# Node tiles in fours, and some gathered rows replaced by columns that VectorE copies, in a two-layer graph network

## The chip, the cores and the metric

The kernel runs on one core of a Trainium2 chip. The metric is device time in microseconds (us) of one execution. PE is TensorE, DVE is VectorE, ACT is ScalarE, POOL is GpSimd and SP is SyncE; PEld is PE's weight load. L12 is line 12 of the kernel that a profile belongs to, so the numbers before and after the change differ.

## The reference

There are 12500 nodes of 128 features and 200000 edges, sorted by destination. `src` is random.

```python
h = jnp.maximum(_layernorm(x, axis=-1), 0.0)
w = edge_weight_raw / jnp.maximum(wsum, EPS)[dst]      # wsum: sum of weights at the edge's destination
feat = jax.nn.relu(h @ W_pool + b_pool)
msg = feat[src] * w[:, None]
neigh = jax.ops.segment_max(msg, dst, num_segments=N)  # 0 where a node has no edge
rst = h @ W1_self + neigh @ W1_neigh + b1
h1 = jax.nn.relu(rst / jnp.maximum(jnp.linalg.norm(rst, axis=1, keepdims=True), EPS))
msg2 = h1[src] * w[:, None]
neigh2 = jax.ops.segment_sum(msg2, dst, num_segments=N) / jnp.maximum(deg, 1.0)[:, None]
out = x + jax.nn.relu(h1 @ W2_self + neigh2 @ W2_neigh + b2)
```

So each layer reads one row of a table for each edge, in random order, reduces the rows of a destination (by maximum, then by weighted sum), and puts two 128x128 products behind it at the nodes.

## The kernel before

The edges are worked in 391 groups of 512 (the last has 320), a group in four chunks of 128 edges; the nodes in 98 tiles of 128. A group ends the edges of some 32 nodes, so four groups complete a node tile. The program is straight-line code, and each engine takes its instructions in the order in which the loops write them. A wait holds everything behind it on its engine.

*Prologue* (to about 290 us). Layer norm, the product with `W_pool`, and the table `feat_d` in DRAM. The normalized features also stay on the chip turned, features on partitions and a node in each column: `h0T`, over the first of two wide tiles (`one_way`). Layer 1 leaves its output as rows in the table `h_d` and turned in `h1T`, over the second (`other_way`). The sums or maxima of the neighbours are gathered in the tile that is not read.

*Layer 1* (to about 2420 us) runs over the groups with index `i`, as a pipeline of several stages in each iteration:

- POOL issues four indirect DMAs (`gather`, L507), each of which fetches the 128 rows of a chunk into a ring of buffers. The first 17 groups take another way. Layer 1's ring starts wide and ends, as buffers are needed elsewhere, with the 11 buffers that layer 2 has too.
- PE transposes the chunks into a PSUM tile `pm` (L896, two buffers), so that an edge is a column. DVE multiplies them by the edge weights `gs`, loaded by SP (L940).
- One iteration later DVE runs a scan with maximum along the edges (L911), which starts again at each new destination (by `kt`) and takes the group before it up by `carry`, a copy of the last column (L929). Two instructions (L933, L936) pick one of each pair of columns into `sc`, and two make selection matrices `sel` (L922).
- PE turns `sc` back into rows (L952, tile `pr`), ACT copies them (L906), PE multiplies them by `sel` (L961), which puts each destination's last value into its column of a window of 48 nodes, and ACT copies the window to its place (L849).
- Node tiles (`nodes1`) come one at a time when their groups are done: two PE products (L747 for the node itself, L743 for the neighbours), the bias on DVE (L757), squares and root on ACT, maximum, reciprocal and scaling on DVE (L764, L765, L773), a PE transpose (L780) and a copy by ACT; two tiles share a store to `h_d`. Side jobs fill gaps.

*Layer 2* (to the end) runs over the groups again. In iteration `i` POOL gathers group `i` from `h_d` into one of 11 buffers; DVE makes a matrix `s` with the edges' weights at their destinations (`places` L996, `weighted` L1001); PE multiplies the rows of group `i-1` by it (`window_product`, L1008, four products in eight passes, tile `pa`, three buffers); DVE adds the result of group `i-2` into the window of `agg2` (`window_add`, L1013), at an address held in a register. These registers are loaded eight at a time (L729).

In four of each 16 groups there is a node tile (`nodes2`): PE products L747 (node), L742 (bias) and L743 (neighbours); L743 needs a `window_add`. In the next iteration DVE applies the ReLU and adds `x` (L802). Four tiles share one load of `x` and one store of `out`.

## Time and profile before

| | |
|---|---|
| median of 3 runs | 4619.21 us (4613.98 to 4619.93) |
| the profiled execution | 4650.7 us, its span 4648.7 us |
| granted PE clock, mean | 0.527 |
| prologue, to 290 us | POOL busy 143.69 us, DVE 156.82, PE 148.17, ACT 133.08 |
| layer 1, 290 to 2420 us | POOL 1347.84, DVE 1306.94, PE 981.70, ACT 282.97 |
| layer 2, 2420 to 4648 us | POOL 1461.81, DVE 278.00, PE 865.25, ACT 0.00 |

The share of busy time is read by stage, as the table does it, since the two layers load DVE very differently. A row of a group of instructions gives line, engine, operation, the tiles written and read, the count, the busy time, the mean length in ns, and the idle time of the engine just before them with what ended it. `remote` stands where the profile shows no instruction of this core that ended at that moment; `issue` where nothing was waited for.

### The profile page before, as it was taken

Reading aid. Unit: us, or ns where it says so; the run is one execution under the profiler, and the core shown is the slowest. Engines: PE = TensorE matmul, PEld = TensorE weight load, DVE = VectorE, ACT = ScalarE, POOL = GpSimd, SP = SyncE. Lnnn points to the kernel's source line nnn. Section 1 sums busy time; section 2 is a strip of 40 time slices with the busy share of each in tenths; the row PEclk is TensorE's granted clock in tenths of the full one; section 3 lists DMA queues with packets and bytes.
Section 4 is the critical chain, followed back from the end, with each engine's and each line's share of the span. In section 5 each row is a group of like instructions: output and inputs, shape, how many; then the busy total and the mean of one; then the engine's idle time right before and its main releaser. Section 6 shows DMA issues by size and latency. Waiting matters only on the chain.

```text
span 4648.7 us, 32678 instructions
## 1 busy us (share of the span) xinstructions
PE 1995.1 (43%) x8700; PEld 1817.3 (39%) x8700; DVE 1741.8 (37%) x5165; ACT 416.0 (9%) x1509; POOL 2953.3 (64%) x3143
## 2 busy tenths in 40 slices
PE   3654543444444444444453344334334333334334
PEld 2444433443434343433342334333334333333334
DVE  3676655765666566665560111111101111111111
ACT  3531111111111111111110000000000000000000
POOL 5356666666666666666646666666666666666665
PEclk8665555555555555555555555555555555555555
DMA  4333443444444444444431112112111111211111
GB/s 130 109 114 116 126 117 103 125 117 114 118 115 120 115 117 116 119 116 117 113 100 46 47 47 62 51 50 56 50 52 53 51 52 51 55 51 52 53 54 45
DMA packets 196303, 397.11 MB, mean 85 GB/s; under 512 B 60703, under 2 KB 69790, under 8 KB 196112
## 3 DMA queue, kind: packets, MB, share of 16 engines
q0 software_dynamic: 100032, 204.97, 17.3%
q1 hardware_dynamic: 95344, 189.06, 13.2%
q8 instruction: 73, 1.20, 0.1%
q10 hardware_dynamic: 736, 0.92, 0.1%
q14 instruction: 118, 0.97, 0.1%
HBM read 374.96 MB, written 19.77 MB: 85 GB/s over the span
## 4 chain that ended last, share of the span: by engine, by line
another core or an unknown queue 23%; issue 23%; PE 20%; POOL 19%; DVE 13%; DMA 1%; ACT 1%; POOLq 0%; ACTq 0%; DVEq 0%
POOL gt L507 18%; PE pa L1008 5%; PE pm L896 5%; DVE pm L911 4%; PE pn L961 4%; DVE pm L940 2%; PE pr L952 2%; DVE sc L936 1%; DVE sc L933 1%; DMA gt<-h_d,srcT 1%; DVE sel L922 1%; PE pn L743 1%; PE pf L643 1%; PE pn L780 1%
## 5 line engine op out<-in xcount | busy, mean ns | idle before, releaser
L507 POOL DMA_INDIRECT gt<-h_d,srcT x1551 | 1463.9, 944 | 743.6 <-issue 419.6
L507 POOL DMA_INDIRECT gt<-feat_d,srcT x1303 | 1230.0, 944 | 680.5 <-issue 294.5
L1008 PE MATMUL pa<-s,gt 128*128 128x24 f32 x3102 | 685.3, 382 | 734.4 <-remote 561.1
L1008 PEld LDWEIGHTS pa<-s,gt 128*128 128x128 f32 x3102 | 682.0, 330 | 748.7 <-remote 567.8
L1013 DVE TENSOR_TENSOR way<-pa,way 128x41 f32 x391 | 78.0, 199 | 1866.9 <-remote 1323.6
L896 PE MATMUL pm<-ident,gt 128*128 128x128 f32 (+1 forms) x1303 | 349.7, 423 | 521.5 <-issue 314.3
L940 DVE TENSOR_TENSOR pm<-pm,gs 128x512 f32<-128x512 f32 x390 | 271.1, 695 | 694.6 <-remote 529.1
L911 DVE TENSOR_TENSOR_SCAN pm<-kt,carry,pm 128x512 f32<-128x512 bf16 x389 | 496.3, 1276 | 4.0
L961 PEld LDWEIGHTS pn<-sel,rows 128*128 128x128 f32 x1564 | 368.8, 324 | 230.8 <-ACT way L849 128.2
L896 PEld LDWEIGHTS pm<-ident,gt 128*128 128x128 f32 (+1 forms) x1303 | 235.8, 218 | 560.4 <-issue 338.5
L961 PE MATMUL pn<-sel,rows 128*128 128x48 f32 x1564 | 358.2, 377 | 217.4 <-ACT way L849 121.9
L743 PE MATMUL pn<-w_2n,way 128*128 128x128 f32 x192 | 74.4, 491 | 601.3 <-issue 325.9
L743 PEld LDWEIGHTS pn<-w_2n,way 128*128 128x128 f32 x192 | 52.8, 323 | 620.2 <-issue 406.6
L906 ACT ACTIVATE rows<-pr 128x256 f32<-128x256 f32 x392 | 149.7, 383 | 1532.8 <-remote 662.1
L952 PE MATMUL pr<-ident,sc 128*128 128x128 f32 x782 | 241.8, 411 | 8.0 <-issue 3.9
L922 DVE TENSOR_SCALAR sel<-cols,lastT,invT 128x48 f32<-128x48 f32 x782 | 243.6, 312 | 0.0
L933 DVE COPY sc<-pm 128x256 f32<-128x256 f32 x391 | 162.6, 416 | 109.5 <-remote 85.9
L952 PEld LDWEIGHTS pr<-ident,sc 128*128 128x128 f32 x782 | 167.2, 224 | 11.5 <-issue 6.1
L936 DVE COPY_PREDICATED sc<-kt,pm 128x256 f32<-128x256 int16 x389 | 168.5, 433 | 4.9 <-issue 4.9
L507 POOL DMA_INDIRECT w2T<-feat_d,srcT x100 | 94.3, 943 | 105.8 <-DVE raw_mv L521 52.0
L780 PE MATMUL pn<-ident,h 128*128 128x128 f32 x94 | 41.9, 446 | 236.8 <-DVE ss L765 73.0
L780 PEld LDWEIGHTS pn<-ident,h 128*128 128x128 f32 x94 | 17.3, 184 | 270.1 <-issue 217.2
(273 smaller groups left out, 2079.6 us busy)
## 6 DMA issues: line engine op xcount, KB each, us to landing
gs<-in_edge_weight SPq DMA_DIRECT2D x389, 256.0 KB
kt<-keep_d SPq DMA_DIRECT2D x97, 512.0 KB
gt<-h_d,srcT POOLq DMA_INDIRECT x1551
gt<-feat_d,srcT POOLq DMA_INDIRECT x1303
feat_d<-fr SPq DMA_DIRECT2D x24, 256.0 KB
xr<-in_x SPq DMA_DIRECT2D x24, 256.0 KB
out<-o SPq DMA_DIRECT2D x24, 256.0 KB
h_d<-h SPq DMA_DIRECT2D x47, 128.0 KB
```

What stands on the lines that cost most here:

```text
L507: nc.gpsimd.indirect_dma_start(out=gt[:k, j, :], out_offset=None, in_=table_d[:, :], in_offset=bass.IndirectOffsetOnAxis(ap=srcT[:k, t, j, ...
L743: nc.tensor.matmul(po, nT, W[neigh_w], start=False, stop=True)
L896: nc.tensor.transpose(pms[i][:, j * P:j * P + k], gt[:k, j, :], ident[:k, :k])
L906: nc.scalar.activation(rws[g][:k, j, :], pr[:k, j, :], AF.Copy)
L911: nc.vector.tensor_tensor_scan(pm[:, :ne], kt[:, :ne], pm[:, :ne], carry, op0=OP.add, op1=OP.max)
L922: nc.vector.tensor_scalar(part, cols[:k, 1, :], lastT[:k, t, j, r:r + 1], invT[:k, t, j, r:r + 1], op0=OP.is_equal, op1=OP.mult)
L933: nc.vector.tensor_copy(sc[:, :ne // 2], two[:, :, 1])
L936: nc.vector.copy_predicated(sc[:, :ne // 2], new[:, :, 1], two[:, :, 0])
L940: nc.vector.tensor_tensor(pms[i][:, :n], rows[:, :n], ws.pop(i)[:, :n], OP.mult)
L952: nc.tensor.transpose(prs[g][:k, j, :], sc[:, j * P:j * P + k], ident)
L961: nc.tensor.matmul(pas[g], rows[:k, j, :], sel[:k, j, :], start=j == 0, stop=j == len(chunks) - 1)
L1008: nc.tensor.matmul(pas[g][:, PART_AT[j]:PART_AT[j] + PART], gt[:k, j, :], s[:k, j, :], start=j == len(chunks) - 1, stop=j == 0, skip_group ...
```

## The change

*Node tiles four at a time.* `quad1` takes the place of `nodes1` for the tiles below 92, `quad2` that of `nodes2` for all full fours. The products are made with features on partitions and four tiles side by side (128x512), so that a bias is a column that ACT adds. `quad1` has the squares summed over the features by a product with a matrix of ones; DVE then runs a maximum, a reciprocal and a product over 128x512. The stages stand in consecutive iterations; a quad comes once in 16 groups.

*PSUM and waits in layer 1.* `pm` has three buffers instead of two, the two `pr` buffers share one tile, the carry is read from the old `pm` instead of a copy, and a group's chunks are transposed in reversed order.

*Columns by DVE.* In layer 1 in every eighth group from 33, and in layer 2 in every third from 13, chunk 1 is not gathered. DVE copies the 128 columns of its source nodes from the turned features that are on the chip. The prologue writes each edge's byte address into a table `at_d` in DRAM (one multiplication and one store for each of four tiles of edges, for both layers); SP loads a chunk's list; a TENSOR_LOAD puts 16 addresses into registers (L751), and eight SCALAR_TENSOR_TENSOR (L800) copy two columns each, with both operands addressed by registers. Each pair comes out as the negative of the first column and the second itself. A chunk takes eight such bursts, spread over its eight or three groups. In layer 1 PE multiplies the columns by `W_pool` straight into `pm`, where ACT applies bias and ReLU with the signs. In layer 2 PE transposes the chunk (L1201, `flip`), and ACT copies it back with the signs, into the buffer that a gather would have filled.

```diff
+    def linear_quad(pn, t, agg, self_w, neigh_w):
+        c = slice(t * P, (t + Q) * P)
+        po = flat(pn())
+        nc.tensor.matmul(po, W[self_w], turned_to[self_w][:, c], start=True, stop=False)
+        nc.tensor.matmul(po, W[neigh_w], agg[:, c], start=False, stop=True)
+        return po
+
+    def quad1(wk, pn, t):
+        po = linear_quad(pn, t, agg1, "1s", "1n")
+        yield
+        sq = wk.tile([P, G], F32, name="sq4", bufs=1)
+        hT = wk.tile([P, G], F32, name="hT4", bufs=1)
+        nc.scalar.activation(sq, po, AF.Square, bias=b1_col)
+        nc.scalar.activation(hT, po, AF.Relu, bias=b1_col)
+        yield
+        ss = flat(pn())
+        nc.tensor.matmul(ss, ones_w, sq, start=True, stop=True)
+        yield
+        nc.scalar.activation(sq, ss, AF.Sqrt)
+        yield
+        c = slice(t * P, (t + Q) * P)
+        nc.vector.tensor_scalar(sq, sq, TINY, None, op0=OP.max)
+        nc.vector.reciprocal(sq, sq)
+        nc.vector.tensor_tensor(turned_to["2s"][:, c], hT, sq, OP.mult)
+        yield
+        ph = pn()
+        for q in range(Q):
+            nc.tensor.transpose(ph[:, q, :], strided(turned_to["2s"], t + q, Q), ident)
+        yield
+        h = wk.tile([P, G], F32, name="sq4", bufs=1).rearrange("p (q d) -> p q d", d=D)
+        nc.scalar.activation(h, ph, AF.Copy)
+        nc.sync.dma_start(runs(h_d, t, Q, Q), in_runs(h, Q))
+
+    def quad2(wk, pn, t, xr):
+        po = linear_quad(pn, t, agg2, "2s", "2n")
+        yield
+        oT = wk.tile([P, G], F32, name="oT4", bufs=1)
+        nc.scalar.activation(oT, po, AF.Relu, bias=b2_col)
+        yield
+        pt = pn()
+        for q in range(Q):
+            nc.tensor.transpose(pt[:, q, :], strided(oT, q, Q), ident)
+        yield
+        o = wk.tile([P, Q, D], F32, name="o4", bufs=2)
+        nc.vector.tensor_tensor(o, pt, xr, OP.add)
+        nc.sync.dma_start(runs(out, t, Q, Q), in_runs(o, Q))
...
@@ in sources(), for each of four tiles of edges @@
+            for layer in range(2):
+                row = (layer * NT + t) * P
+                place = wk.tile([P, G], I32, name="sa")
+                nc.vector.tensor_scalar(place, sr[:, t, :], 4.0, float(TABLES_AT[layer]), op0=OP.mult, op1=OP.add)
+                nc.sync.dma_start(at_d[row:row + P, :], place)
+                yield
...
@@ class Columns @@
+            while (g := first + int(len(self.place) * every)) < end:
+                part = len(self.place) * every % 1 if even else 0
+                self.place[g] = len(self.place) % 2
+                span = min(every, within)
+                begin = g - int(span) - lead
+                steps = P // BURST
+                for turn, step in ((begin - 2, self.load), *((g + k, step) for k, step in after)):
+                    self.plan.setdefault(turn, []).append((step, g, 0))
+                for k in range(steps):
+                    turn = begin + int(k * span / steps + part)
+                    self.plan.setdefault(turn, []).append((self.fetch, g, k * BURST))
...
+    def two_by_two(slot, r, columns_read):
+        for e in range(0, BURST, 2):
+            nc.vector.scalar_tensor_tensor(slot[:, r + e:r + e + 2], zero_high, columns_read[e],
+                                           columns_read[e + 1].to_broadcast([P, 2]),
+                                           op0=OP.subtract, op1=OP.min)
...
@@ layer 1 @@
+        for k, engine, copy, j, every, first in ((0, mybir.EngineType.DVE, two_by_two, 1, 8, FIRST + 16),):
...
+            def multiplied(g, _, j=j, slot=slot):
+                nc.tensor.matmul(pms[g][:, j * P:(j + 1) * P], W["pool"], slot(g), start=True, stop=True)
...
-                gts[i] = gather(buffer(i, True), feat_d, i)
+                gts[i] = gather(buffer(i, True), feat_d, i, besides=bycol)
...
-                pms[i] = ps.tile([P, G], F32, name="pm", bufs=2)
+                pms[i] = ps.tile([P, G], F32, name="pm", bufs=3)
...
-                if g + 1 < NG:
-                    carry = wk.tile([P, 1], F32, name="carry")
-                    nc.vector.tensor_copy(carry, pm[:, ne - 1:ne])
+                carry = pm[:, ne - 1:ne]
...
@@ layer 2 @@
+        for k, engine, copy, j, every, first in ((0, mybir.EngineType.DVE, two_by_two, 1, 3, 13),):
...
+            bycol.append(Columns(engine, copy, False if k else None, other_way, 1, lists_of(k), slot,
+                                 ((-2, turned), (0, back)), 4, j, every, first, NG - 5, True, 5))
...
-                gts[i] = gather(buffer(i, False), h_d, i)
+                gts[i] = gather(buffer(i, False), h_d, i, besides=bycol)
                 places(i)
+            for c in bycol[:1]:
+                c.ahead()
+                c.fetch_one(i)
...
+            quad_stage(1)
+            quad_stage(3)
+            for c in bycol[:1]:
+                c.ahead()
+                c.fetch_one(i)
...
                 window_add(g, window_at(mybir.EngineType.DVE, g))
```

On DVE, two consecutive groups in the middle of layer 2 read like this before (`way_64` is `agg2`, `place` the comparison with the places in the window, `s` the weighted matrix):

```order
L1013 ISA
L1013 TENSOR_TENSOR way_64<-pa,way_64 128x41
L996 TENSOR_TENSOR place<-place,locT 128x96
L1001 TENSOR_TENSOR s<-place,w2T 128x96
L1013 ISA
L1013 TENSOR_TENSOR way_64<-pa,way_64 128x41
```

The same engine in the changed kernel, from one window add to the next (`listed` is the list of addresses, `way_66` the turned features, `gt_109` a buffer of the ring; L1214, L1219 and L1231 are the former L996, L1001 and L1013):

```order
L1231 TENSOR_TENSOR way_65<-pa,way_65 128x41
L751 TENSOR_LOAD listed
L800 SCALAR_TENSOR_TENSOR gt_109<-b_80,way_66 128x2 x8
L1214 TENSOR_TENSOR place<-place,locT 128x96
L751 TENSOR_LOAD listed
L800 SCALAR_TENSOR_TENSOR gt_109<-b_80,way_66 128x2 x8
L1219 TENSOR_TENSOR s<-place,w2T 128x96
L751 TENSOR_LOAD listed
L800 SCALAR_TENSOR_TENSOR gt_109<-b_80,way_66 128x2 x8
L844 TENSOR_LOAD bases
L1231 ISA
L1231 TENSOR_TENSOR way_65<-pa,way_65 128x41
```

Between two window adds there are now up to three bursts, each a load and eight copies, all behind the first add and ahead of the second; with eight bursts in three groups, some iterations have two.

On PE, a place in layer 2 where node tiles begin reads like this before (`gt_` buffers of successive groups, `w_2s`, `w_2n` the weights of the layer):

```order
L1008 MATMUL pa<-s,gt_101 128x24 x4
L747 MATMUL pn<-w_2s,way_65 128x128
L742 MATMUL pn<-b_81,ident 128x128
L743 MATMUL pn<-w_2n,way_64 128x128
L1008 MATMUL pa<-s,gt_102 128x24 x4
L747 MATMUL pn<-w_2s,way_65 128x128
L742 MATMUL pn<-b_81,ident 128x128
L743 MATMUL pn<-w_2n,way_64 128x128
L1008 MATMUL pa<-s,gt_103 128x24 x4
```

The same engine at such a place in the changed kernel:

```order
L1201 MATMUL flip<-ident,gt_103 128x128
L905 MATMUL pn<-way_66,w_2s 128x512
L906 MATMUL pn<-way_65,w_2n 128x512
L1226 MATMUL pa<-s,gt_101 128x24 x4
L1226 MATMUL pa<-s,gt_102 128x24 x4
L1226 MATMUL pa<-s,gt_103 128x24 x4
L945 MATMUL pn<-ident,oT_41836 128x128 x4
L1201 MATMUL flip<-ident,gt_106 128x128
L1226 MATMUL pa<-s,gt_104 128x24 x4
```

The products of four tiles stand together ahead of one group's product instead of three by three ahead of four, the transposes of the quad follow three groups later, and in every third group a fetched chunk is turned.

More of the change, by code (lines that the diff above doesn't have):

```diff
@@ L500, in edges_of, with gather @@
         return *divmod(g, P), ne, [(j, min(P, ne - j * P)) for j in range(-(-ne // P))]
-    def gather(gt, table_d, g, only=None, last=None):
+    def gather(gt, table_d, g, only=None, last=None, besides=()):
         t, r, ne, chunks = edges_of(g)
@@ L506, in gather @@
         for j, k in chunks if only is None else chunks[only:only + 1]:
+            if any(c.j == j and c.takes(g) for c in besides):
+                continue
             nc.gpsimd.indirect_dma_start(
@@ L975, in gnn_kernel @@
                 side_step()
+            for c in bycol:
+                c.turn(i, c.load, c.fetch)
         assert not busy
@@ L1079, in gnn_kernel @@
                 window_add(g, window_at(mybir.EngineType.DVE, g))
-        assert late is None
+            for c in bycol[:1]:
+                c.ahead()
+            for c in bycol:
+                c.turn(i, c.turned)
+            for c in bycol[1:]:
+                c.fetch_one(i)
+            for c in bycol:
+                c.turn(i, c.back)
+            for c in bycol:
+                c.turn(i, c.fetch)
+        assert late is None and not quads
     both.close()
```

159 lines of the change are left out of this document (143 added, 16 removed).

## The prediction

> **What bounds the kernel now.** I read the page first (busy shares, chain, costliest groups), then the table of stretches, then one line at a time, then the timeline of one period of layer 2.
>
> ```profile
> PE 1995.1 (43%) x8700; PEld 1817.3 (39%) x8700; DVE 1741.8 (37%) x5165; ACT 416.0 (9%) x1509; POOL 2953.3 (64%) x3143
> another core or an unknown queue 23%; issue 23%; PE 20%; POOL 19%; DVE 13%; DMA 1%; ACT 1%; POOLq 0%; ACTq 0%; DVEq 0%
> L507 POOL DMA_INDIRECT gt<-h_d,srcT x1551 | 1463.9, 944 | 743.6 <-issue 419.6
> L507 POOL DMA_INDIRECT gt<-feat_d,srcT x1303 | 1230.0, 944 | 680.5 <-issue 294.5
> ```
>
> POOL is the busiest engine at 64%, and it does almost nothing but issue gathers: four of 128 rows in each group. The chain of waits ends on no single engine, so POOL is not simply the bound; something also holds it up. The next views are the table of stretches (start and end, length, then busy us and count of PE, PEld, DVE, ACT, POOL) for a middle piece of layer 1 and of layer 2, and POOL's line in the second piece.
>
> ```profile
> 700.00:2200.00 1500.00, 679.91 (x3003) 607.83 (x3003) 916.04 (x2281) 193.33 (x813) 969.30 (x1027) 0.52 0.42 117
> 2500.00:4500.00 2000.00, 780.28 (x3436) 751.67 (x3435) 242.36 (x1159) 0.00 (x0) 1324.86 (x1404) 0.50 0.19 52
> L507 POOL DMA_INDIRECT gt<-h_d,srcT x1404: 938/944/1148, 2503.4 to 4496.8; - x176
>   issue: 380.3, 1243
>   remote: 224.1, 78
> ```
>
> Layer 2 passes 1404 gathers in 2000 us, 1.425 us each, or 5.70 us a group of four; layer 1 1027 in 1500 us, 1.46 each. Of this 0.944 is the gather and 380.3/1243 = 0.31 us the gap that always follows: 1.25 us, 4.99 a group, if nothing stopped it. The rest is some 78 stalls of 3 us, one every 26 us. From the page's two groups, idle less 0.30 for each gather: 743.6 - 465 = 278 us of stalls in layer 2, 680.5 - 391 = 290 us in layer 1. VectorE is busy for 12% of layer 2 and 61% of layer 1.
>
> What stalls POOL shows in the timeline (start, length, engine, line, and in brackets the idle time before) and in the groups of layer 2.
>
> ```profile
> 3262.89 10.41 PE L1008 MATMUL pa<-s,gt 128*128 128x24 f32 x48 [12.12 <-remote]
> 3289.35 0.20 DVE L1013 TENSOR_TENSOR way<-pa,way 128x41 f32 x1 [12.71 <-remote]
> 3289.61 0.84 PE L743 MATMUL pn<-w_2n,way 128*128 128x128 f32 x2 [15.26 <-issue]
> 3262.36 0.94 POOL L507 DMA_INDIRECT gt<-h_d,srcT  x1 [4.48 <-remote]
> 3307.10 0.94 POOL L507 DMA_INDIRECT gt<-h_d,srcT  x1 [5.12 <-remote]
> 3308.32 0.20 DVE L1013 TENSOR_TENSOR way<-pa,way 128x41 f32 x1 [18.30 <-remote]
> 3319.36 0.94 POOL L507 DMA_INDIRECT gt<-h_d,srcT  x1 [2.50 <-PE pn L742]
> L1013 DVE TENSOR_TENSOR way<-pa,way 128x41 f32 x354 | 70.6, 199 | 1682.4 <-remote 1220.1 <-PE pa L1008 279.8 <-issue 117.3
> L1008 PE MATMUL pa<-s,gt 128*128 128x24 f32 x2806 | 619.8, 382 | 639.9 <-remote 521.3 <-issue 60.4 <-DVE s L1001 30.6
> L743 PE MATMUL pn<-w_2n,way 128*128 128x128 f32 x174 | 68.0, 494 | 566.1 <-issue 320.8 <-DVE way L1013 192.9 <-DMA gt<-h_d,srcT 52.4
> ```
>
> PE's products of the first row end at 3273.3, yet VectorE's window add L1013, which needs the last of them, starts at 3289.35, sixteen us later, while POOL issues without a break; the next comes 1.2 us after a POOL stall of 5.12. So VectorE learns late that PE is done, mostly when POOL pauses. PE, in step with VectorE, then frees the ring of 11 buffers in batches (48 products = six groups in 10.4 us), and POOL stops when the ring is full. Node tiles make it worse: L743 needs VectorE's add, and VectorE's next add needs PE again. PE's idle time before L743 is 566 us against 640 before L1008, though node tiles come in only 4 of 16 groups. In this period of 16 groups POOL stalls 4.2, 4.8 and 2.2 us beyond its gap, the last two, 63%, among the four node tiles.
>
> **The change, part by part.** The sum is against the profiled execution's own 4650.7 us, which is 0.7% above the median of 4619.21 (ratio 0.9932).
>
> *Gathers removed.* Layer 1 has columns in groups 33, 41 ... 385 (45), layer 2 in 13, 16 ... 385 (125): 170 of POOL's 3143 instructions. At POOL's undisturbed 1.25 us: layer 2 **-156**, layer 1 **-56**. If POOL's pace of 1.43 holds in proportion it is -179 and -66; if the ring's consumer sets the pace, 0 and 0. I take 1.25, the part that POOL certainly no longer spends.
>
> *Node tiles by four, layer 2.* Four round trips L743 - L1013 in 16 groups become one, spread over four iterations. The stalls at stake are 63% of 278 = 175 us; none may go, since the stall before 3262.36 came without a node tile. I take 40%, **-70** (0 to -175): the other late signals stay and will refill some of it.
>
> *Layer 1: tiles by four, a third `pm` buffer, no carry copy.*
>
> ```profile
> L757 DVE TENSOR_TENSOR r<-pn,b 128x128 f32<-128x128 f32 x64 | 17.9, 280 | 0.0
> L773 DVE TENSOR_SCALAR h<-r,ss 128x128 f32<-128x128 f32 x66 | 19.5, 295 | 2.3
> L765 DVE RECIPROCAL ss<-ss 128x1 f32<-128x1 f32 x66 | 10.8, 164 | 2.3
> L764 DVE TENSOR_SCALAR ss<-ss 128x1 f32<-128x1 f32 x66 | 9.9, 150 | 0.0
> L338 DVE RECIPROCAL r_f<-r_f x4: 952/953/954, 135.1 to 739.4; 128x128 f32<-128x128 f32 x4
> L940 DVE TENSOR_TENSOR pm<-pm,gs 128x512 f32<-128x512 f32 x260 | 180.9, 696 | 502.5 <-remote 398.7 <-PE pm L896 30.8 <-issue 26.6
> L929 DVE COPY carry<-pm 128x1 f32<-128x1 f32 x261 | 42.6, 163 | 0.0
> ```
>
> VectorE gave four tiles 4 x (280 + 295 + 164 + 150) = 3.56 us. A quad's reciprocal of 128x512 is four of L338's, 3.8 us, and the maximum and product some 0.7 each as L940: 5.2 us, or 1.6 more in 16 groups. The carry copy gives back 16 x 0.07 (what its successor starts later), 1.1. VectorE waits 502.5 us before L940 in this piece, about 31 in 16 groups, which covers it; were it uncovered, 23 quads would cost 23 x 5.2 = 120. Of the 290 us of stalls the shorter round trips may take some: **-30**, a tenth (-290 to +120). The chunk straight into `pm` swaps a transpose for a product of the same size, and its two ReLUs go to ScalarE, busy for 13% here: 0.
>
> *VectorE's fetch.* A chunk is 8 loads of 16 registers and 64 SCALAR_TENSOR_TENSOR of 128x2.
>
> ```profile
> L729 DVEq TENSOR_LOAD <-bases x49: 593/596/1056, 2430.3 to 4625.9; - x49
> L1041 DVEq TENSOR_LOAD <-bases x3: 308/309/314, 2543.4 to 2755.5; - x3
> 161.94 0.16 DVE L530 SCALAR_TENSOR_TENSOR raw_off<-raw_mv,raw_rstd 128x4 f32<-128x4 f32 x1
> 162.02 0.28 DVE L520 BATCH_NORM_STATS2 raw_st<-gt 128x6 f32<-128x128 f32 x1
> L802 DVE SCALAR_TENSOR_TENSOR o<-pn,xr 128x128 f32<-128x128 f32 x86 | 24.2, 281 | 0.0
> 3263.07 0.27 DVE L996 TENSOR_TENSOR place<-place,locT 128x96 f32<-128x96 f32 x1 [0.17 <-issue]
> 3263.66 0.27 DVE L996 TENSOR_TENSOR place<-place,locT 128x96 f32<-128x96 f32 x1
> ```
>
> Eight registers take 596 ns, one 309: 41 ns for each further one, so 16 take 0.92 us (two loads of eight, 1.19, is the upper end). The nearest small instruction, L530, lets its successor start after 80 ns; L802, much larger, takes 281. I take 80, as the sizes 128x4 and 128x2 are close: a burst is 0.92 + 8 x 0.08 = 1.56 us, a chunk **12.5 us** (at 281 ns and nothing overlapped 8 x (0.92 + 2.25) = 25.3; at 80 ns with loads wholly under other work 5.1). VectorE's own work in a group of layer 2 is 0.59 us (the two L996 rows), 1.8 in three. So three groups need 14.3 us of VectorE, 13.7 of POOL's bare issuing (11 x 1.25), and passed in 17.1 until now. That fits, but tightly.
>
> The bursts stand in the in-order queue behind L1013 that waits for PE. In the time in which VectorE now sits there (1682 of 2000 us), the work behind it is not done, and after the signal it has 14.3 us to catch up with in three groups instead of 1.8. PE's products, and POOL through the ring, wait for that. The nearest row gives only bounds: 0 if a burst ahead of L1013 fills the wait, hundreds of us if the waits add (third rival). I take **+40**, a fifth of the 208 us of layer 2's stalls left above. In layer 1 a burst goes into each of eight groups with its load behind the scan (L1111), which is long enough (1.28 us) to hide it; eight instructions of 0.08 to 0.13 are some 1 us on a VectorE with 2.2 us free in a group: 0.
>
> A rule of the Trainium skill speaks against this part. Its page "Runtime: NRT & Kernel Launch", section "Instruction fetch mechanics", puts a register load at about 200 ns per register even in bulk. By it 16 registers take 3.2 us, a chunk 30.7, and layer 2 is bound by VectorE at about 10.8 us a group, +1.9 ms by that estimate. L729 against L1041 says 41 ns, and the measurement decides.
>
> *The rest.* The flip transpose and its copy (125 products of L743's size, 0.49 us, on a PE that is idle for 61% of layer 2; ScalarE has nothing else there) come two groups ahead of use: 0, or 125 x 0.49 = 61 uncovered. SP's 170 list loads are issued two groups before the first burst, behind stores of tiles on the same queue: 0 as long as such a store waits under 10 us. The address lists in the prologue, 8 multiplications of 128x512 at some 0.69 (as L940) and 8 stores beside other work: **+5** (0 to 20).
>
> **Sum:** -156 - 56 - 70 - 30 + 40 + 5 = -267; 4650.7 - 267 = 4384, times 0.9932 = **4354 us**. Layer 2 would pass at 5.70 - 186/391 = 5.22 us a group.
>
> **Rivals.**
> 1. *The gathers were hidden.* PE's idle time before L1008 is put to `remote` and VectorE, none of it to a landing gather, so data are there when PE comes, and the pace may be that of the exchange between PE and VectorE. Then only -70 - 30 + 5 remain: 4556, **4525 us**. Against it: POOL itself fills 1.25 of 1.43 us, and signals are late just while it issues. Chance 0.17.
> 2. *The stalls of layer 2 go altogether,* as VectorE is no longer parked and PE's round trips are spread. The floor is then VectorE's 14.3 us in three groups, 4.77 each: 0.93 x 375 = -349, with layer 1's -86 and +5: 4221, **4192 us**. For it: most stalls of the period shown lie at the node tiles. Against: the one before 3262.36 does not. Chance 0.14.
> 3. *VectorE becomes the bound of layer 2: slower.* Point of decision: a burst above (17.1 - 1.8)/8 = 1.91 us. If each fetching instruction holds the queue for 199 ns, as the register-addressed L1013 is long, a burst is 2.51, three groups 21.9, a group 7.30: +1.60 x 375 = +600, with -86 and +5: 5170, **5135 us**. For it: no row shows these instructions in a row, and L1013's address comes from a register too. Against: L530's 80 ns. Chance 0.11.
> 4. *Each register costs a load of its own,* 309 ns as L1041: 4.94 us for 16, (8 x (4.94 + 0.64) + 1.8)/3 = 15.5 us a group, +9.8 x 375, some **8.2 ms**. Only if L729's 596 for eight does not go on to sixteen. Chance 0.01. The figure of the Trainium skill's page "Runtime: NRT & Kernel Launch", weighed above, would lie between L729 and this.
>
> **How the numbers follow.** The forecast has 0.57, its own range 4230 to 4460 (-70 and -30 each from nothing to double, the fetch 0 to +100). With rivals 1 and 2 the range is **4150 to 4550**; rivals 3 and 4 and the tails stay out. A measurement of this kernel can tell about 0.2% from no change. Faster by more: forecast and rivals 1 and 2 but for their tails, 0.86; within 0.2%: 0.02; slower: 0.12.
>
> **What would show it.** Burst: spacing of L800 and the length of L751 (0.92 expected). POOL: L525 in layer 2 at 1.33 us each and fewer `remote` stalls; at 1.43 with 11 gathers rival 1 is out too, as the pace is then POOL's own. Node tiles: PE's idle before the quad's products well under the 566 us of L743. Rival 3 shows as a VectorE that is busy or loading throughout layer 2 and POOL stalling for most of its time. I would be most wrong if VectorE's wait at L1231 and its bursts add up instead of overlapping.

## The result

The changed kernel takes 4667.4 us (4643.06 to 4677.91, 6 runs) where the kernel before takes 4619.57: ratio **1.0103** (1.0082 to 1.0124), slower by 1.0%. The forecast was 4354 us, the range 4150 to 4550. Its profiled execution took 4670.77 us, its span 4669.0. First the page's rows of the changed kernel.

```profile
PE 2045.8 (44%) x8256; PEld 1663.9 (36%) x8256; DVE 3295.4 (71%) x15299; ACT 488.3 (10%) x1472; POOL 2796.9 (60%) x2973
DVE 37%; issue 27%; PE 17%; another core or an unknown queue 11%; POOL 3%; DVEq 3%; ACT 1%; DMA 0%; ACTq 0%; POOLq 0%
L800 DVE SCALAR_TENSOR_TENSOR gt<-b,way 128x2 f32<-128x2 f32 x10560 | 1585.0, 214 | 703.3 <-issue 682.2
L525 POOL DMA_INDIRECT gt<-h_d,srcT x1426 | 1346.6, 944 | 871.2 <-PE pa L1226 412.8
```

Its two stretches in the middle of the layers (start and end, length, then busy us and count of PE, PEld, DVE, ACT, POOL):

```profile
700.00:2200.00 1500.00, 715.66 (x2947) 555.55 (x2947) 1233.99 (x3978) 207.95 (x705) 969.47 (x1025) 0.55 0.42 118
2500.00:4500.00 2000.00, 798.34 (x3180) 691.92 (x3180) 1306.32 (x8508) 56.13 (x137) 1206.61 (x1279) 0.50 0.18 48
```

POOL issues 170 gathers less, and the chain of waits has moved from POOL (19%, now 3%) to DVE (13%, now 37%). Layer 2 passed 1404 gathers in 2000 us, now 1279: at 11 instead of 12 in three groups that is 5.73 us a group, against 5.70. What was taken from POOL it now spends standing: 871.2 - 0.30 x 1426 = 443 us of stalls in layer 2, against 278. Layer 1 did gain: 1025 gathers at 31 in eight groups are 5.67 us a group, against 1500/1027 x 4 = 5.84.

Where VectorE's time goes in layer 2 shows in the rows of that stretch.

```profile
L800 DVE SCALAR_TENSOR_TENSOR gt<-b,way 128x2 f32<-128x2 f32 x7423 | 1125.3, 215 | 569.3 <-issue 549.5 <-DMA gt<-h_d,srcT 1.1
L1214 DVE TENSOR_TENSOR place<-place,locT 128x96 f32<-128x96 f32 x351 | 90.7, 258 | 55.1 <-issue 37.3 <-DVE way L1231 17.4
L1219 DVE TENSOR_TENSOR s<-place,w2T 128x96 f32<-128x96 f32 x351 | 87.1, 248 | 25.9 <-issue 25.4
L1231 DVE TENSOR_TENSOR way<-pa,way 128x41 f32 x351 | 67.5, 192 | 30.6 <-issue 17.0 <-PE pa L1226 13.2
L751 DVEq TENSOR_LOAD <-listed x929: 1093/1097/1418, 2501.1 to 4499.8; - x186
```

VectorE waited 1682 us for PE at its window add and now 30.6. In 2000 us it is busy for 1306 and idle for some 570 before L800, and that idle time is nearly all `issue`: the profile shows no signal that VectorE waits for, and yet its next copy does not start. In this trace VectorE is the bound of layer 2.

The same shows in the timeline of the changed kernel (some of the rows of L800; VectorE's other instructions are left out).

```profile
3302.70 1.13 DVE L800 SCALAR_TENSOR_TENSOR gt<-b,way 128x2 f32<-128x2 f32 x8
3306.76 0.22 DVE L800 SCALAR_TENSOR_TENSOR gt<-b,way 128x2 f32<-128x2 f32 x1 [0.51 <-issue]
3307.46 0.22 DVE L800 SCALAR_TENSOR_TENSOR gt<-b,way 128x2 f32<-128x2 f32 x1 [0.48 <-issue]
3308.16 0.35 DVE L800 SCALAR_TENSOR_TENSOR gt<-b,way 128x2 f32<-128x2 f32 x2 [0.48 <-issue]
3308.87 0.22 DVE L800 SCALAR_TENSOR_TENSOR gt<-b,way 128x2 f32<-128x2 f32 x1 [0.36 <-issue]
3309.56 0.35 DVE L800 SCALAR_TENSOR_TENSOR gt<-b,way 128x2 f32<-128x2 f32 x2 [0.47 <-issue]
3310.29 0.22 DVE L800 SCALAR_TENSOR_TENSOR gt<-b,way 128x2 f32<-128x2 f32 x1 [0.37 <-issue]
3317.36 1.14 DVE L800 SCALAR_TENSOR_TENSOR gt<-b,way 128x2 f32<-128x2 f32 x8 [0.35 <-issue]
```

Eight copies take 1.13 us in the first and last rows, 0.13 from one to the next. In between many start 0.70 us apart, though each is as short as ever. I sorted the distances inside bursts between 2500 and 4400 us by the time since POOL last resumed after a pause (an idle time over 1.3 us, where 0.30 is usual). While POOL issues, the mean distance is 0.14 us in the first 8 us, 0.15 from 8 to 10, 0.37 from 10 to 12, and 0.60 from 12 to 16. Copies get slow when POOL has issued for some ten microseconds without a pause; of the 569 distances over 0.4 us, 18 lie in the first 8 us.

The other loss is at the start. POOL's longest wait up to 300 us in the changed kernel (total us, times, longest):

```profile
POOL r_f L525 <- DVE b L810: 82.0, 1, 82.0
```

Four successive scans and a gather of POOL in its timeline:

```profile
289.18 1.29 DVE L1111 TENSOR_TENSOR_SCAN pm<-kt,pm 128x512 f32<-128x512 bf16 x1
317.71 1.28 DVE L1111 TENSOR_TENSOR_SCAN pm<-kt,pm 128x512 f32<-128x512 bf16 x1
345.18 1.29 DVE L1111 TENSOR_TENSOR_SCAN pm<-kt,pm 128x512 f32<-128x512 bf16 x1
376.19 0.94 POOL L525 DMA_INDIRECT gt<-feat_d,srcT  x1 [10.87 <-remote]
378.48 1.28 DVE L1111 TENSOR_TENSOR_SCAN pm<-kt,pm 128x512 f32<-128x512 bf16 x1
```

The same four scans (groups 21 to 24) in the timeline of the kernel before:

```profile
312.25 1.28 DVE L911 TENSOR_TENSOR_SCAN pm<-kt,carry,pm 128x512 f32<-128x512 bf16 x1
315.84 1.28 DVE L911 TENSOR_TENSOR_SCAN pm<-kt,carry,pm 128x512 f32<-128x512 bf16 x1
320.06 1.29 DVE L911 TENSOR_TENSOR_SCAN pm<-kt,carry,pm 128x512 f32<-128x512 bf16 x1
325.93 1.29 DVE L911 TENSOR_TENSOR_SCAN pm<-kt,carry,pm 128x512 f32<-128x512 bf16 x1
```

L810 belongs to `sign_tiles`, which the change runs on VectorE in iteration 17 of layer 1, with a tile that is also the buffer of group 19. So POOL holds group 19's gather, and all behind it, for 82 us. Then it fills the long ring in one run, from 253 to 365 us, and while it does, one group passes in 28 to 33 us instead of 4 to 6.

### The profile page after: what moved, and what is told of

Same layout as the page of the kernel before. It is cut to its first block, busy times and chain, and to the rows that moved or that the text cites. A ratio compares the mean times of both kernels' runs of the same rounds, so it can differ in the third digit from the quotient of the medians.

```text
span 4669.0 us, 42924 instructions
## 1 busy us (share of the span) xinstructions
PE 2045.8 (44%) x8256; PEld 1663.9 (36%) x8256; DVE 3295.4 (71%) x15299; ACT 488.3 (10%) x1472; POOL 2796.9 (60%) x2973
## 4 chain that ended last, share of the span: by engine, by line
DVE 37%; issue 27%; PE 17%; another core or an unknown queue 11%; POOL 3%; DVEq 3%; ACT 1%; DMA 0%; ACTq 0%; POOLq 0%
DVE gt L800 13%; PE pa L1226 10%; DVE pm L1111 7%; DVE pm L1140 4%; DVEq L751 3%; DVE sel L1122 3%; DVE sc L1136 2%; DVE sc L1133 2%; POOL gt L525 1%; DVE sq L925 1%; PE pm L1096 1%; PE pn L1162 1%; PE pn L906 1%; PE two_pr L1153 1%
## 5 line engine op out<-in xcount | busy, mean ns | idle before, releaser
L800 DVE SCALAR_TENSOR_TENSOR gt<-b,way 128x2 f32<-128x2 f32 x10560 | 1585.0, 214 | 703.3 <-issue 682.2
L525 POOL DMA_INDIRECT gt<-h_d,srcT x1426 | 1346.6, 944 | 871.2 <-PE pa L1226 412.8
L525 POOL DMA_INDIRECT gt<-feat_d,srcT x1263 | 1195.3, 946 | 660.1 <-issue 343.2
L1226 PE MATMUL pa<-s,gt 128*128 128x24 f32 x3102 | 717.1, 385 | 1259.5 <-issue 1104.9
L1226 PEld LDWEIGHTS pa<-s,gt 128*128 128x128 f32 x3102 | 692.2, 328 | 1340.3 <-issue 1228.5
L1111 DVE TENSOR_TENSOR_SCAN pm<-kt,pm 128x512 f32<-128x512 bf16 x389 | 498.1, 1280 | 32.1 <-issue 31.8
L1153 PE MATMUL two_pr<-ident,sc 128*128 128x128 f32 x782 | 243.4, 412 | 510.3 <-ACT rows L1106 272.5
L1153 PEld LDWEIGHTS two_pr<-ident,sc 128*128 128x128 f32 x782 | 125.5, 201 | 629.0 <-issue 317.3
L1106 ACT ACTIVATE rows<-two_pr 128x256 f32<-128x256 f32 x392 | 149.5, 382 | 1241.4 <-remote 714.4
L789 ACT ACTIVATE gt<-flip,b 128x128 f32<-128x128 f32 x125 | 45.8, 367 | 1741.2 <-PE flip L1201 1004.8
L1214 DVE TENSOR_TENSOR place<-place,locT 128x96 f32<-128x96 f32 x391 | 101.0, 258 | 61.7 <-issue 42.8
L1219 DVE TENSOR_TENSOR s<-place,w2T 128x96 f32<-128x96 f32 x391 | 97.2, 249 | 29.4 <-issue 28.4
L1231 DVE TENSOR_TENSOR way<-pa,way 128x41 f32 x391 | 75.3, 193 | 56.6 <-PE pa L1226 23.4
```

What stands on the lines that cost most here:

```text
L525: nc.gpsimd.indirect_dma_start(out=gt[:k, j, :], out_offset=None, in_=table_d[:, :], in_offset=bass.IndirectOffsetOnAxis(ap=srcT[:k, t, j, ...
L800: nc.vector.scalar_tensor_tensor(slot[:, r + e:r + e + 2], zero_high, columns_read[e], columns_read[e + 1].to_broadcast([P, 2]), op0=OP.su ...
L1106: nc.scalar.activation(rws[g][:k, j, :], pr[:k, j, :], AF.Copy)
L1111: nc.vector.tensor_tensor_scan(pm[:, :ne], kt[:, :ne], pm[:, :ne], carry, op0=OP.add, op1=OP.max)
L1153: nc.tensor.transpose(prs[g][:k, j, :], sc[:, j * P:j * P + k], ident)
L1226: nc.tensor.matmul(pas[g][:, PART_AT[j]:PART_AT[j] + PART], gt[:k, j, :], s[:k, j, :], start=j == len(chunks) - 1, stop=j == 0, skip_group ...
```

## The experiments

The labels are those of the expectations. Each job ran on one chip, beside the kernel before, and the jobs differ: the kernel before takes 3944 us in one of them and 4612 in another. I call a job or its chip quick where the kernel before takes about 3950 us, and late where it takes 4612 to 4650. Each ratio is to the kernel before in the same job. The kind need not belong to the chip: the same chip number, 4, stands beside a late job (before_again to e5_spare_4) and a quick one (e13 and e14).

### Four edits, apart

```diff
@@ e1_spare: another tile for the signs @@
-                sign_tiles(work("f1")[:, :P])
+                sign_tiles(wk.tile([P, D], F32, name="r", bufs=2))
@@ e2_none_in_2: no columns in layer 2 @@
-        for k, engine, copy, j, every, first in ((0, mybir.EngineType.DVE, two_by_two, 1, 3, 13),):
+        for k, engine, copy, j, every, first in ():
@@ e3_every_4 @@
-        for k, engine, copy, j, every, first in ((0, mybir.EngineType.DVE, two_by_two, 1, 3, 13),):
+        for k, engine, copy, j, every, first in ((0, mybir.EngineType.DVE, two_by_two, 1, 4, 13),):
@@ e4_none_in_1: no columns in layer 1 @@
-        for k, engine, copy, j, every, first in ((0, mybir.EngineType.DVE, two_by_two, 1, 8, FIRST + 16),):
+        for k, engine, copy, j, every, first in ():
```

> The changed kernel, but the small tile in which the signs are prepared no longer shares memory with the buffer of group 19. Theory: POOL's wait of 82 us at 170 us for DVE's L810 is this sharing alone; without it POOL starts its long run of gathers while the first 17 groups are still worked on, and the crawl of one group in 28 us between 267 and 376 us goes. Scan 30 then starts at 340 to 365 us instead of 418, and the kernel takes 4667 - 60 = 4607 us (4585 to 4620). Rival: the crawl belongs to any long uninterrupted run of gathers and only moves; then scan 30 stays after 400 us and the kernel within 15 us of 4667.

> The changed kernel, but layer 2 gathers every chunk again (no columns there; node tiles in fours stay). Theory: VectorE with its bursts is the bound of layer 2 (17.2 us in three groups), so without them layer 2 is paced by POOL as before, less what the node tiles in fours save: 5.4 to 5.6 us a group instead of 5.73, the kernel 4540 to 4620 us. Rival: POOL is still the bound and the 125 gathers are really saved, the gain only being lost elsewhere; then it takes 4667 + 156 = 4820 us.

> The changed kernel, but in layer 2 VectorE fetches a chunk in every fourth group instead of every third (94 instead of 125 chunks). Theory: VectorE is the bound with every third; with every fourth it needs 8 x 1.93 + 4 x 0.6 = 17.8 us in four groups, 4.5 a group, POOL 15 gathers at 1.43, 5.36 a group, so POOL is the bound again and layer 2 takes some 5.4 a group: 4667 - 0.33 x 391 = 4540 us (4510 to 4600). Rival: what costs is each exchange between PE, ScalarE and VectorE for a fetched chunk or the bursts' place ahead of the window add; with a quarter fewer chunks and 31 more gathers the kernel then stays within 30 us of 4667.

> The changed kernel, but layer 1 gathers every chunk again (no columns there). Theory: POOL paces layer 1, 45 gathers come back at 1.25 to 1.46 us each: 4667 + 56 to + 66, so 4725 us, the stretch from scan 50 to scan 380 longer by some 50 us. Rival: VectorE's bursts cost layer 1 as much as the gathers save; then within 15 us of 4667.

The kernel before took 3944.06 us here, and all four expectations missed in their absolute times. Ratios: e1 0.9479 (0.9463 to 0.9494), e2 1.0075 (1.0058 to 1.0092), e3 0.9781 (0.9764 to 0.9797), e4 0.9827 (0.9810 to 0.9843). The changed kernel itself came to such a chip later (`after_third`): 0.9679. Against that each edit can be read, to some 9 us as the two jobs differ: without the false wait 79 us less, without columns in layer 2 156 us more, with every fourth group 40 more, without columns in layer 1 58 more. So the differences that e1 and e4 expected came out nearly as stated, and e2 went to its rival. e3 fits neither of its two: its theory had 127 us less, its rival at most 30 either way. The forecast's price of a gather holds here to a few microseconds: 125 x 1.25 = 156, 31 x 1.25 = 39, 45 x 1.25 = 56. The theory that VectorE is the bound of layer 2 falls on such a chip.

### The same kernels again, and every fourth group

e5_spare_4 puts the edits of e1 and e3 together; e1_again is e1, before_again and after_again are the two kernels themselves.

> The kernel before, once more, with a trace of its own. In the first four experiments it took 3944 us, not 4619, and in their traces POOL issued a gather every 1.25 us without a stall while PE's signals came 0.2 us after its products. Theory: the 250 to 290 us of POOL stalls in each layer of the first trace are late signals from PE that come with the chip and not with the kernel. If this run takes about 3944 us, its trace shows POOL at 1.25 us a gather in both layers, 4.99 us a group, PE's idle time ended by landing gathers, and no wait of VectorE for PE over 5 us. Rival: the kernel before had the stalls there as well and only its other work was faster; then its trace shows POOL at 1.3 us or more a gather. If it takes about 4619 us, the trace is as the first.

> The changed kernel, once more, beside the kernel before. Theory: where the kernel before takes 3944 us, POOL's 82 us of waiting before group 19 cost 80 us in full (3737 without it), so this takes 3737 + 80 = 3820 us, ratio 0.968, layer 2 at 11/3 x 1.25 = 4.58 us a group. Rival: VectorE's bursts are the bound of layer 2 here too, and the ratio is 1.00 or more, as first measured. Where the kernel before takes 4619 us: ratio 1.01.

> The changed kernel with the tile of the signs apart from group 19's buffer, beside the changed kernel itself. Theory: 75 to 85 us less than the changed kernel in the same job where the kernel before takes 3944 us; where it takes 4619 us 40 to 80 us less, ratio 0.993. Rival: no difference over 15 us.

> The same with a fetched chunk in every fourth group of layer 2 instead of every third. Theory where the kernel before takes 3944 us: POOL is the bound of layer 2, 15/4 x 1.25 = 4.69 instead of 4.58 us a group, 40 us slower than with every third. Theory where it takes 4619 us: VectorE, slowed there to 17.2 us in three groups, is relieved, 60 to 130 us faster than with every third. Rival for both: no difference over 15 us.

This chip was like the first: the kernel before took 4612.44 us, and before_again 1.0004 of that, so its question was not answered. after_again 1.0114 (1.0095 to 1.0133), e1_again 0.9972 (0.9953 to 0.9990), e5_spare_4 0.9807 (0.9778 to 0.9835). Taking the false wait away is worth 64 us (from 4663 to 4599), and fewer fetched chunks are worth another 69, though 31 gathers come back. The expectations held, but for e1_again's ratio of 0.993. e1's own numbers, made for a late chip, can be compared here as well: scan 30 was to start at 340 to 365 us and the kernel to take 4585 to 4620. In e1_again it starts at 348 us (in after_again at 417), so the crawl goes with the shared tile and does not only move. In layer 2 VectorE is overloaded here, on the quick chip it is not. POOL's longest waits up to 300 us in e1_again, where L810 is gone from the list:

```profile
POOL w2T L525 <- DVE raw_mv L539: 37.7, 1, 37.7
POOL gt L525 <- issue: 18.3, 62, 0.3
```

VectorE's rows in layer 2 of e5_spare_4 (2500 to 4300 us):

```profile
L800 DVE SCALAR_TENSOR_TENSOR gt<-b,way 128x2 f32<-128x2 f32 x5212 | 817.6, 216 | 585.7 <-issue 575.8
L1214 DVE TENSOR_TENSOR place<-place,locT 128x96 f32<-128x96 f32 x328 | 87.0, 265 | 132.8 <-issue 94.7 <-DVE way L1231 37.3
L1231 DVE TENSOR_TENSOR way<-pa,way 128x41 f32 x328 | 63.2, 193 | 41.6 <-issue 27.6 <-PE pa L1226 13.1 <-PE flip L1201 0.5
```

Even with a quarter fewer copies VectorE still loses 585.7 us before them: the mean distance inside a burst rises to 0.26 us, from 0.20 in e1_again, so the slow distances take part of what the smaller work leaves. Layer 2 then passes at 5.51 us a group (window adds 50 to 350), not at 5.36 as POOL's pace alone would have it.

### What the fetch costs without gathers, and what the node tiles are worth

All four have the signs' tile apart. e6 has no columns in layer 2, e8 has them in every fifth group, e9 in every fourth and none in layer 1 (edits as above). e7 leaves the gathers of layer 2 out from group 14 on:

```diff
@@ e7_no_gathers @@
-                gts[i] = gather(buffer(i, False), h_d, i, besides=bycol)
+                gts[i] = buffer(i, False) if i >= 14 else gather(buffer(i, False), h_d, i, besides=bycol)
```

> Signs' tile apart, and no columns in layer 2, so that of the change only node tiles in fours act there. Where the kernel before takes 4612 us (signals late): theory, node tiles in fours take 70 us off layer 2 as forecast, layer 2 passes in 2137 us against 2207 before and the kernel in 4510 us; rival, the stalls come back elsewhere, layer 2 takes 2207 us, the kernel 4580 us. Where the kernel before takes 3944 us: POOL is the bound with 12 gathers in three groups, 4.98 us a group, 3737 + 156 = 3893 us by either.

> Signs' tile apart, every third group as in the change, but layer 2 issues no gathers from group 14 on (PE multiplies old rows; the output is not the reference's). It asks whether VectorE's slow copies and PE's late signals need POOL's issuing. Theory: yes; then the copies follow each other in 0.13 us throughout, VectorE waits for no signal over 2 us, and layer 2 is bound by VectorE at 4.0 to 4.5 us a group on any chip, against 5.7 with gathers where the kernel before takes 4612 us. Rival: slow copies come from VectorE's own instruction supply or from loading registers; then the spells of 0.7 us a copy stay and layer 2 stays above 5.0 us a group there.

> Signs' tile apart, a fetched chunk in every fifth group of layer 2. Where the kernel before takes 4612 us: theory, VectorE is no longer the bound with every fourth and each gather more costs POOL's pace, 19/5 x 1.43 = 5.43 us a group; as every fourth came to 5.51 and not 5.36, VectorE still costs a little there, so within 25 us of every fourth (4530). Rival: VectorE's slow spells still bind with every fourth; then 30 to 60 us faster than with it. Where it takes 3944 us: 4.73 us a group, 60 us slower than with every third (3737).

> Signs' tile apart, every fourth group in layer 2, no columns in layer 1. Theory: POOL's pace rules layer 1, so its 45 gathers cost 45 x 1.25 to 1.46 = 56 to 66 us over the kernel with them (4530 us where the kernel before takes 4612). Rival: there, VectorE's bursts cost layer 1 as much as the gathers; within 15 us. Where the kernel before takes 3944 us VectorE was busy for 96% of layer 1 with columns, and it can even be faster without them.

The kernel before took 4650.09 us. e6 0.9926 (0.9910 to 0.9943), e7 0.8761 (0.8744 to 0.8778), e8 0.9761 (0.9745 to 0.9778), e9 0.9938 (0.9921 to 0.9955). Three rows of e7 in layer 2 (2600 to 3900 us):

```profile
L800 DVE SCALAR_TENSOR_TENSOR gt<-b,way 128x2 f32<-128x2 f32 x6489 | 924.8, 215 | 176.9 <-issue 171.3
L1226 PE MATMUL pa<-s,gt 128*128 128x24 f32 x2437 | 564.9, 385 | 565.7 <-DVE s L1219 559.0 <-DVE way L1231 6.7
L1231 DVE TENSOR_TENSOR way<-pa,way 128x41 f32 x306 | 59.5, 194 | 0.8 <-issue 0.7
```

VectorE's window add in layer 2 of e6 (2500 to 4300 us), and PE's products there for the groups and for the quads (2500 to 4500 us):

```profile
L1231 DVE TENSOR_TENSOR way<-pa,way 128x41 f32 x319 | 63.2, 198 | 1329.8 <-remote 954.7 <-PE pa L1226 195.6 <-issue 164.6
L1226 PE MATMUL pa<-s,gt 128*128 128x24 f32 x2834 | 612.3, 377 | 1109.7 <-remote 769.6 <-issue 303.6 <-PE pa L1226 18.9
L906 PE MATMUL pn<-way,w_2n 128*128 128x512 f32 x44 | 42.7, 1073 | 152.4 <-DVE way L1231 99.9 <-issue 43.5 <-DVE o L948 9.0
```

e7 settles the slow copies. With POOL silent, on a chip where they are slow with gathers (602 of 3656 distances inside bursts over 0.4 us in e8, 2500 to 4300 us), 5660 of 5676 (2600 to 3900 us) are 0.12 to 0.14 us, and layer 2 passes at 4.25 us a group, 12.8 in three. The wait of 0.8 us at the window add says little about PE's signals, as VectorE always has work ahead of it here. ScalarE shows them: its copy L789 starts at most 0.09 us after the transpose that it waits for, where in e8 half of such starts are over 1 us late, the latest 14.4. So both the slow copies and the late signals need POOL's gathers; VectorE's own instruction supply and its register loads (1096 ns here too) are not the cause by themselves. e7 takes away the issuing and the transfers at once, so which of the two does it is not shown. With gathers the same work took 17.2 us.

e6 went to the rival: without columns, VectorE waits for PE's late signals in layer 2 as before (1329.8 of 1800 us), and layer 2 takes 2208 us from the first to the last window add, against 2207 and 2200 in the two traces of the kernel before; this chip is at most 0.8% slower, so at most some 15 us are gained. The quads did what they were made for: PE's idle time before the node tiles' product with the neighbours falls from 566 us (L743) to 152 (L906). But the time comes back before the groups' products, where 640 us (L1008) become 1110 (L1226). The whole kernel gains 34 us. On the quick chip e2 agrees (+30 us, of which -58 and +79 are accounted for).

What the columns of layer 1 bring on a late chip is not clear. e9 against e5 is 0.0131 of 4612, 60 us, as its theory had it, but these are two chips. On one chip scans 50 to 380 take 1880 us in e9 and 1860 to 1861 in e6, e7 and e8, which have the 41 columns: 20 us, where the quick chip gives 51 (1652 in e4, 1601 in after_third).

e8 came out better than every fourth (e5) by 0.0046, inside the 25 us that its theory allowed, on another chip. On its own chip it passes from scan 380 to the end in 2215 us where e9, with every fourth, takes 2274; that is the rival's figure, so the two stay undecided. The same chip shows what the columns of layer 2 can be worth: e8 fetches 75 of them and takes 74 us less than e6, which fetches none (4538.68 and 4612.63).

### Nothing in the gathers' place, and a shorter ring

```diff
@@ e10_nothing_for_it, e13: e1, and in layer 2 @@
+        taken, bycol = bycol, []
...
-                gts[i] = gather(buffer(i, False), h_d, i, besides=bycol)
+                gts[i] = gather(buffer(i, False), h_d, i, besides=taken)
@@ e11_spare_ring9, e14: e1, and (e12 with every fifth group) @@
-            return full[g % len(full)]
+            return full[g % 9]
```

> Signs' tile apart; layer 2 leaves out chunk 1's gather in every third group and puts nothing in its place (no lists, no bursts, no flip; PE multiplies old rows, the output is not the reference's). Against the kernel with the bursts, 4599 us where the kernel before takes 4612, it prices the fetch; against the one that gathers all chunks, ratio 0.9926, it prices the 125 gathers. Theory: 125 gathers are worth 156 to 179 us by themselves, layer 2 passes at 5.15 to 5.25 us a group and the ratio is 0.955 to 0.96, so the fetch takes all of it back through slow copies. Rival: PE's late signals set the pace whatever POOL has to issue; then layer 2 stays at 5.5 to 5.6 us a group, ratio 0.98 or more. Where the kernel before takes 3944 us: 4.58 us a group, as with bursts (3737), since POOL is the bound.

> Signs' tile apart, every third group, but layer 2's ring has 9 buffers instead of 11. Copies are slow (0.7 us each) once POOL has issued for some 10 us without a pause. Theory: with two buffers less POOL fills the ring sooner, pauses sooner and oftener, fewer copies are slow, and layer 2 gets shorter by 30 to 100 us (ratio 0.975 to 0.99 instead of 0.9972). Rival: the ring's length sets only how far POOL is ahead, its runs last as long as the signals are late; then the ratio stays 0.99 to 1.005. Where the kernel before takes 3944 us nothing changes (3737).

> The same ring of 9 with a fetched chunk in every fifth group. Theory as there: below the 0.9761 measured with 11 buffers by 0.005 to 0.02. Rival: as with 11 buffers or slower, as POOL, not VectorE, is the bound here and a shorter ring makes it wait more. Where the kernel before takes 3944 us: 4.73 us a group, as with 11.

> The changed kernel once more, as its ratio has been seen only where the kernel before takes 4612 us and more: 1.010 to 1.011 is expected there. Where it takes 3944 us: 3737 + 80 = 3820 us, ratio 0.968.

> e10 once more, since it met a chip without late signals, where it could not tell its theories apart. Where the kernel before takes 4612 us: theory, the 125 gathers are worth 156 to 179 us by themselves, layer 2 passes at 5.15 to 5.25 us a group, ratio 0.955 to 0.96; rival, PE's late signals set the pace whatever POOL has to issue, 5.5 to 5.6 us a group, ratio 0.98 or more. Where it takes 3944 us: 0.947 again.

> e11 once more, for the same reason. Where the kernel before takes 4612 us: theory, POOL pauses sooner and oftener with 9 buffers, fewer copies are slow, ratio 0.975 to 0.99 instead of 0.9972; rival, 0.99 to 1.005. Where it takes 3944 us: 0.948 again.

Both jobs met chips of the quick kind, where the kernel before takes 3952.01 and 3943.55 us: e10 0.9472 and e13 0.9474, e11 0.9479 and e14 0.9476, e12 0.9632 (0.9616 to 0.9648; 50 gathers more than e1 at 1.25 us are 0.0158 of it), after_third **0.9679** (0.9663 to 0.9695). There e10 and e11 differ by nothing from e1 (0.9479): the fetch is free, since POOL is the bound. What they were made for, the worth of the 125 gathers by themselves and the length of POOL's runs where signals are late, they could not tell. Three rows of after_third in layer 2 (2200 to 3600 us):

```profile
L525 POOL DMA_INDIRECT gt<-h_d,srcT x1119 | 1059.4, 947 | 341.0 <-issue 313.5 <-DMA gt<-h_d,srcT 23.5 <-PE pa L1226 2.7
L800 DVE SCALAR_TENSOR_TENSOR gt<-b,way 128x2 f32<-128x2 f32 x6502 | 938.3, 217 | 193.6 <-issue 174.8
L1226 PE MATMUL pa<-s,gt 128*128 128x24 f32 x2442 | 562.7, 382 | 713.4 <-DMA gt<-h_d,srcT 619.0 <-DVE place L1214 40.3 <-DVE gt L800 34.1
```

POOL's longest wait up to 300 us in the same run:

```profile
POOL r_f L525 <- DVE b L810: 85.6, 1, 85.6
```

The same program, with instructions as long as on the first chip: POOL has no idle time but its own gap (341.0/1119 = 0.30 us), PE waits for landing gathers, and VectorE's copies cost 193.6 us of idle time for 6502 instead of 569.3 for 7423. The wait for the signs' tile is nearly the same on both kinds (85.6 and 82.0 us).

## Why the prediction was wrong

- **The fetch, +40,** was the step that turned the sign. I had put POOL's disturbance down to late signals of PE alone, from which VectorE's own instructions would be free. They are not: with copies 0.7 us apart after some 10 us of POOL's issuing, three groups took 17.2 us, which is rival 3's point of decision, a burst of 1.91, reached by another mechanism than L1013's 199 ns. Where nothing disturbs it, three groups take 12.8 us (e7) against 14.3 forecast, but that nearness is luck: the load is 1.10 us instead of 0.92 and a copy 0.13 instead of 0.08, so that added up as in the forecast a burst would be 2.14, and only the loads that hide under other work, which the 12.5 us of a chunk had left out, make up for it. In the ratios to the kernel before, e6 without columns has 0.9926 and e1 with every third group 0.9972, so columns in layer 2 cost 21 us net (on two chips, to some 12 us) where -156 + 40 was forecast. That the loss lies in how many are fetched, and not in fetching, e8 shows: 75 columns gain 74 us.
- **"The address lists in the prologue ... +5"** sized what the edit computes and not what it holds. `sign_tiles` is a handful of small instructions, but its scratch tile is group 19's buffer, so POOL waits 82 us: +64 us on a late chip, +79 on a quick one. I followed the changed order on DVE and PE, and did not ask which tile each new instruction writes and who next writes it.
- **Node tiles in layer 2, -70:** nothing of it is seen. The sign that I had named came, PE's idle time before the quad's products is far under 566 us, yet e6's layer 2 is as long as before: the stalls at the four node tiles were where late signals were met, not their source, and all of it refilled. The 63% of the stalls came from one period with three of them. **Layer 1's -30** is not seen apart: on one chip (before_again, after_again) scans 50 to 380 take 41 us less, with columns and quads together.
- **The gathers, -156 and -56,** are exact where POOL is free: 156 (e2) and 58 us (e4). On a late chip the columns of layer 1 are worth between 20 us (one chip) and 60 (two chips), and those of layer 2 about 1 us each when every fifth group has one (e8). Whether layer 2's 125 are worth anything there without a fetch stays open.
- Where the time went on one late chip, by the traces of before_again and e1_again: up to layer 2's first window add 38 us less (-86 + 5 forecast), from there to the end 24 us more (-186 forecast). The shared tile adds 58 between the traces of e1_again and after_again, together +44; the medians say +51. On a quick chip e1's 0.9479 is near the forecast's 4354/4619 = 0.943, again by luck: 206 us are gained, the 170 gathers alone are 212, and neither the -100 of the node tiles nor the +40 is in it.
- The Trainium skill's 200 ns per register for a load (page "Runtime: NRT & Kernel Launch", section "Instruction fetch mechanics") would have made the load 3.2 us; L751 took 1097 ns for 16 on every chip, 69 each, 63 for each beyond L729's eight. The measurement is nearer to the trace of before than to that, though not the 41 that I drew from it. The same page explains such loads as loads from HBM, and `listed` is a tile on the chip, so its figure may not be meant for them.

## What to carry to other kernels

For every new instruction, ask whose memory its output shares and which queue is next in line for that memory: a moment of setup in a borrowed buffer can hold a prefetching engine for as long as the engine that runs them lags behind it. When a trace shows one engine's signals late only while another issues DMAs without a pause, price any new work on a third engine under the same disturbance, and leave it slack: with every fifth group and the signs' tile apart the kernel took 0.9761 of before on a chip of the late kind, where every third took 0.9972; with the shorter ring as well, every fifth took 0.9632 on a chip of the quick kind. The slack has its price there, since every third with the signs' tile apart and the same ring took 0.9479. And measure in more than one job before a gain of a few per cent is believed, since this change is 1% slower on one kind of chip and 3.2% faster on another.

## What the runs showed of the hardware

The kernel before takes 3944 or 3952 us in three jobs and 4612 to 4650 in three (the first comparison among them). It has no trace of a quick job, so the two kinds are compared by the changed kernels: their instructions are as long in both (a gather 944 to 947 ns), and the difference is what stands between them. In the quick jobs POOL's gathers follow each other at 1.25 us for the whole of layer 2, and VectorE's window add starts in the median 0.04 us after the product that it waits for (e2, by the ends that the profile gives). In the late ones signals come up to some 16 us later (first trace of the kernel before), and VectorE's copies start 0.7 us apart, once POOL has issued for about 10 us. Without gathers both vanish on such a chip (e7). What makes the jobs differ no run here shows. As chip number 4 was late in one job and quick in another, it may be a state that comes and goes on one chip; whether the number means the same chip both times is not known.
